# A transformer block's last steps reordered: written order on all engines in the end, a receptance, a key and values in other steps, normalising on VectorE

## The chip, the cores and the metric

The kernel runs on one core of a Trainium2 chip. The metric is device time in microseconds (us) of one execution, start to end; lower is better. A core has TensorE (matrix products and transposes, called PE in the profile), VectorE (DVE), ScalarE (ACT), GpSimd (POOL) and SyncE (SP), which here only issues DMA transfers. Each engine works through its own instructions in their order and waits on semaphores for the others.

## The reference

Eight sequences of 1024 tokens with 256 features, all in float32. A block of two halves, each behind a layer normalisation that is scaled and shifted by a vector of the batch; the gates `ga` and `gb` are vectors of the batch as well:

```python
h = _layernorm(x) * (1 + ca) + sa
x = x + ga * attention(h)          # 16 heads of 16, causal softmax, projection w_out, bias
h = _layernorm(x) * (1 + cb) + sb
# channel mixing; x_prev is h shifted by one token
xr = mu_r * h + (1 - mu_r) * h_prev
xk = mu_k * h + (1 - mu_k) * h_prev
r = sigmoid(xr @ W_r.T)
x = x + gb * r * (square(relu(xk @ W_k.T)) @ W_v.T)
```

## The kernel before

A batch's tokens are cut into two blocks `(b, c)` of 512 (`CW`); a block is four tiles of 128 tokens. The attention is worked through in 32 units `u`, one for four heads of one batch: unit 30 and 31 are the last two of batch 7, so `u // 4` is the batch.

**Steps.** A unit has nine entries (`ORDER`): five pieces along the diagonal (a to e) and four whole tiles of keys (0 to 3). For the last two units other pieces (f, g, h, i) replace b, c and d, so that all of block 0 comes first. A step takes one entry twice: for unit `S`, the *maxima* (`maxima`: products `pp` of queries and keys on TensorE into PSUM, their row maxima on VectorE), and for an earlier entry `T`, nine steps behind (`LAG`), the *weights* (`weights`: products `pw` with the maxima folded in, exponentials on ScalarE, and on GpSimd a select that clears what lies above the diagonal). One entry before `T` is `T1`: at the end of a group of entries, `attend` sums weights times values into `po`. So the steps from 290 to 298 have weights but no maxima, and behind step 298 comes the last `attend`.

When a unit's sums of one block are complete, they have to be divided by the row sums. For units 30 and 31 that is `turn_sums` (four transposes `psum`, a reciprocal and a copy `wide` on VectorE), and one step later `gather_last` (products `pinv`, a multiplication on VectorE, four transfers into `oT`, those of the very last block on the queues of SP and ScalarE alternately).

**Fill.** The rest of the block's work is written into the steps by hand. In `POST_LAST` and `END` an entry `20 x.value0` puts the function `value0` of block `x` twenty steps behind step 261. In `POST_LAST`, `x` and `y` are the two blocks of batch 6; in `END`, `x` and `y` are blocks 0 and 1 of batch 7. A step's fill runs behind its products and before `T1`'s sums; names that begin with `norm` are put ahead of the step's other fill. What a block goes through, in this order: `project0`/`project2` (products `py` with the folded output weights, added to `xb` on VectorE; 0 and 2 are the first of two token tiles), `stats0`/`stats1` (statistics on VectorE, a power and two small multiplications on GpSimd), `norm0`/`norm1` (normalising), `turn` (eight transposes `ptb`, two copies with scale and shift to `h2T`), `mix` (differences of neighbours on GpSimd), four `mixed` (VectorE, into `mix` for the receptance and `step` for the keys), `receptance0`/`2` (products `pr`, tanh on ScalarE to `r`), `key0`/`1` (products `pk`, relu on ScalarE, square on GpSimd to `ka`), `value0`/`2` (`multiplied`: products `pkv`; `valued`: r times them on VectorE, the addition to `xb` on GpSimd, and behind `value2` the transfer to `out`). What `soon` holds is done in a later step, ahead of that step's fill.

In a step with no maxima and no fill TensorE makes five transposes of the identity ("heat").

**Order and banks.** The wrapper `InOrder` ties each instruction to the one before on its engine. TensorE always keeps the written order; the other four keep it where `strict[0]` or `start[0]` is set. `strict[0]` is set in the steps and cleared before the end; there the tile framework's own planner puts the instructions of the four engines in an order. PSUM has four banks tagged `t` (`bank`: pw, po, ptb, psum, pinv) and two double banks tagged `s` (pp). From step 290 on `late[0]` is set, and `bank_apart` (py, pr, pk, pkv, heat) takes its banks from `s`, which no maxima need any more; before it takes them from `t`.

**The end.** `tail` handles block (7, 1) after all steps, in halves of 256 tokens: `project`, `normal`, `turned`, `mixed_half`, `receptance`, `keys`, `values`, with the other block's `multiplied` and `valued` in between. Its tiles end in `_last`. Behind the last sums and before `tail` come `turn_sums`, `gather_last` and the keys of block (7, 0), in the order of `soon`.

Of the kernel before, what the change touches and what calls it, by code (L numbers as in the profile page):

```python
# [8 lines left out]
F32 = mybir.dt.float32  # L9
AF = mybir.ActivationFunctionType  # L10
ALU = mybir.AluOpType
# [3 lines left out]
P = 128  # L15
B, N, D = 8, 1024, 256
H, HD = 16, 16
DC = D // P
CW = 512
NC = N // CW  # L20
# [52 lines left out]
def adaln_block(  # L73
# [89 lines left out]
    def tokens(ap, b, c):  # L163
        return ap[b, c * CW : (c + 1) * CW, :].rearrange("(t p) d -> p t d", p=P)
# [202 lines left out]
    def normalise(xt, S, tag, half):  # L367
        if half == 0:
            S["h"] = sb.tile([P, NT, D], F32, tag="h", bufs=2, name=f"h{tag}")
        h, mv, rs = S["h"], S["mv"], S["rs"]  # L370
        for t in (2 * half, 2 * half + 1):
            if strict[0]:
                act.activation(
                    h[:, t, :],
                    xt[:, t, :],
                    AF.Identity,
                    bias=S["away"][:, t : t + 1],
                    scale=rs[:, t : t + 1],
                )
            else:  # L380
                dve.tensor_scalar(
                    h[:, t, :],
                    xt[:, t, :],
                    mv[:, t, 0:1],
                    rs[:, t : t + 1],
                    ALU.subtract,
                    ALU.mult,
                )

    def transposed(h, to, b, d, shift, scale, name):  # L390

        pt = bank(name)
        for t in range(NT):
            pe.transpose(
                pt[:, t * P : (t + 1) * P], h[:, t, d * P : (d + 1) * P], ident
            )
        by, at = modT[:, scale, d, b : b + 1], modT[:, shift, d, b : b + 1]
        if d and shift == SHIFT_A:
            dve.tensor_scalar(to, pt, by, at, ALU.mult, ALU.add)
        else:  # L400
            act.activation(to, pt, AF.Identity, bias=at, scale=by)
# [363 lines left out]
    def post(b, c):  # L765
# [57 lines left out]
        def receptance(t0):  # L823
            pr = bank_apart(f"pr{b}_{c}_{t0}")
            rows(pr, S["mix"], wr_sb, (t0, t0 + 1))
            r = sb.tile([P, CW], F32, tag="r", bufs=2, name=f"r{b}_{c}_{t0}")
            act.activation(r, pr, AF.Tanh, scale=0.5)
            S["r", t0] = r

# [28 lines left out]
        def tail(other):  # L858

            def both(f):
                f(0)
                f(1)

            def columns(half):
                return slice(half * CW // 2, (half + 1) * CW // 2)

            both(lambda half: project(2 * half))
            other["multiplied0"]()  # L870
            st = sb.tile([P, NT, 6], F32, tag="st", bufs=2, name="st_last")
            mv = sb.tile([P, NT, 2], F32, tag="mv", bufs=2, name="mv_last")
            rs = sb.tile([P, NT], F32, tag="rs", bufs=2, name="rs_last")
            h = sb.tile([P, NT, D], F32, tag="h", bufs=2, name="h_last")

            def normal(half):
                ts = (2 * half, 2 * half + 1)
                for t in ts:
                    dve.bn_stats(st[:, t, :], S["x"][:, t, :])
                    dve.bn_aggr(mv[:, t, :], st[:, t, :])  # L880
                of = slice(2 * half, 2 * half + 2)
                dve.tensor_scalar_add(rs[:, of], mv[:, of, 1], EPS)
                pool.tensor_tensor(rs[:, of], rs[:, of], m_half[:, of], ALU.pow)
                if half:
                    pool.tensor_mul(away, mv[:, of, 0], rs[:, of])
                    pool.tensor_scalar_mul(away, away, -1.0)
                for n, t in enumerate(ts):
                    if half:
                        act.activation(
                            h[:, t, :],  # L890
                            S["x"][:, t, :],
                            AF.Identity,
                            bias=away[:, n : n + 1],
                            scale=rs[:, t : t + 1],
                        )
                        continue
                    dve.tensor_scalar(
                        h[:, t, :],
                        S["x"][:, t, :],
                        mv[:, t, 0:1],  # L900
                        rs[:, t : t + 1],
                        ALU.subtract,
                        ALU.mult,
                    )

            away = sb.tile([P, 2], F32, tag="away", bufs=2, name="away_last")
            both(normal)
            h2T = sb.tile([P, DC, CW + 1], F32, tag="h2T", name="h2T_last")
            pool.tensor_copy(h2T[:, :, 0:1], A[b, 0]["edge"])

            def turned(half):
                pt = bank(f"pt_last{half}")
# [13 lines left out]
                        scale=modT[:, SCALE_B, d, b : b + 1],  # L926
                    )

            turned(0)
            other["multiplied2"]()  # L930
            turned(1)
            step = sb.tile([P, DC, CW], F32, tag="step", name="step_last")
            S["mix"] = sb.tile([P, DC, CW], F32, tag="mix", bufs=2, name="mix_last")

            def mixed_half(half):
                of = columns(half)
                for d in range(DC):
# [5 lines left out]
                for n in range(2):  # L943
                    for d in range(DC):
                        dve.scalar_tensor_tensor(
                            (S["mix"], step)[n][:, d, of],
                            step[:, d, of],
                            mus[:, n, d : d + 1],
                            h2T[:, d, of],
                            ALU.mult,  # L950
                            ALU.add,
                        )

            both(mixed_half)
            other["valued0"](), other["valued2"]()
            S["ka"] = sb.tile([P, DC, CW], F32, tag="mix", bufs=2, name="ka_last")

            def keys(half):
                of = columns(half)
# [11 lines left out]
                act.activation(ka, pk, AF.Relu)  # L971
                dve.tensor_mul(ka, ka, ka)

            both(lambda half: (receptance(2 * half), keys(half)))

            def values(half):
                t0 = 2 * half
                pv = bank(f"pkv_last{half}")
                rows(pv, S["ka"], G[b]["wv"], (t0, t0 + 1))
                r = S["r", t0]  # L980
                dve.scalar_tensor_tensor(r, r, 1.0, pv, ALU.add, ALU.mult)
                dve.tensor_add(flat(t0), flat(t0), r)
                (sync, act)[half].dma_start(
                    tokens(out, b, c)[:, t0 : t0 + 2, :], S["x"][:, t0 : t0 + 2, :]
                )

            both(values)

        return dict(
            load=load_xb,  # L990
# [26 lines left out]

    soon = []

    def step(T, T1, S, now, fill):  # L1020


# [21 lines left out]
        for f in fill:  # L1044
            f()
        if not S and not fill:

            pt = bank_apart(f"heat{now}")
            for n in range(5):
                pe.transpose(pt[:, :P], ident, ident)  # L1050
        if T1 and T1[1] in groups_of(T1[0]):
            finish(T1, now)
        if S:
# [64 lines left out]
    12 y.stats0; 13 x.mixed01; 13 x.mixed10; 13 x.receptance0; 14 x.mixed11; 15 x.receptance2;  # L1118
    15 y.stats1; 16 y.norm0; 17 x.key0; 17 y.norm1; 18 x.key1; 18 y.turn; 19 y.mix; 20 x.value0;
    20 y.mixed00; 21 y.mixed01; 21 y.mixed10; 22 x.value2; 22 y.mixed11; 22 y.receptance0;  # L1120
    23 y.receptance2; 24 y.key0; 25 y.key1; 26 y.value0; 27 y.value2
    """
    PREP = """
    -9 m.stats0; -8 m.stats1; -6 m.norm0; -4 m.norm1; -3 m.turn; -2 n.stats0; 0 n.stats1; 1 m.q0;
# [11 lines left out]
    22 m.k1; 22 n.q1; 24 n.k1; 26 n.v0; 28 n.v2  # L1136
    """
    END = """
    16 x.load; 18 x.bias; 26 y.load; 28 x.project0; 28 y.bias; 29 x.project2; 30 x.stats0;
    30 x.stats1; 31 x.norm0; 32 x.norm1; 32 x.turn; 33 x.mix; 34 x.mixed00; 34 x.mixed01;  # L1140
    34 x.mixed10; 34 x.mixed11; 35 x.receptance0; 36 x.receptance2
    """

    def place(table, at, **of):
# [32 lines left out]
    for b in range(B):  # L1177
# [10 lines left out]
            fold0=lambda b=b: fold(b, 0),  # L1188
            fold1=lambda b=b: fold(b, 1),
        )  # L1190
    place(END, at, x=ready[b][0], y=ready[b][1])


    mask = const.tile([P, CW], F32, tag="mask", name="mask")
# [53 lines left out]
        )  # L1248
    strict[0] = False
    finish(order_t[-1], len(slots))  # L1250
    for n, f in ((1, "key0"), (2, "key1")):
        soon.append((len(slots) + n, ready[B - 1][0][f]))
    soon.sort(key=lambda z: z[0])
    strict[0] = True
# [59 lines left out]
```

## Time and profile before

| | |
|---|---|
| median of 3 runs | 1411.76 us (1409.19 to 1415.02) |
| profiled execution | 1412.37 us, span 1410.7 us, mean granted TensorE clock 0.995 |
| busy: PE, DVE, ACT, POOL | 1382.5, 1063.3, 894.7, 550.9 us |
| step 290 begins (first pw_h) | 1335.64 us |
| last po_i ends | 1374.81 us |
| first py that waits for oT | 1382.79 us |
| last product pkv_last ends | 1405.76 us |
| last transfer to out is issued | 1407.30 us |

The profile is of one execution. Its page gives the span, the busy time of each engine, 40 equal slices of the span and the chain of work that ended last. Beside the page the trace answers with the instructions in order of time (start, length, engine, tile out<-in, shape, count, and in brackets the idle time before and what ended it) and with the busy time of each engine, the granted TensorE clock and the share of the DMA engines in any stretch. Every instruction stands at line 123, that of the wrapper; groups are told apart by their tiles.

### The profile page before, as it was taken

To read this page: it belongs to the slowest core of one execution; us is meant where nothing else is said; L and a number is where in the kernel's file an instruction comes from. 1 tells how busy PE (TensorE), PEld (TensorE's weight loads), DVE (VectorE), ACT (ScalarE), POOL (GpSimd) and SP (SyncE) were. 2 spreads that over 40 slices of the span, in tenths; PEclk is the share of its full clock that TensorE was granted. 3 is DMA by queue.
4 is the path that set the end of the run, shared out by engine and by line. 5 is a ranking of instruction groups with operands and counts; after the bars stand their busy time and mean duration, and the time that the engine had idled before them with its cause. 6 is when DMAs were issued, how large, how long until landed. Compare 5 with 4: busy or idle time off the path is not lost.

```text
span 1410.7 us, 29817 instructions
## 1 busy us (share of the span) xinstructions
PE 1382.5 (98%) x11285; PEld 758.2 (54%) x11285; DVE 1063.3 (75%) x2872; ACT 894.7 (63%) x1695; POOL 550.9 (39%) x841
## 2 busy tenths in 40 slices
PE   9999999999999999999999999999999999989997
PEld 5544555555555555555554555556555555555545
DVE  6777687788777878788877787778887886878524
ACT  3466666666666666666666666666666666566561
POOL 1142242435423454334534355234643344345431
PEclk9999999999999999999999999999999999999999
DMA  6512423222222323223242222323231232301101
GB/s 192 182 36 79 132 77 114 62 97 82 86 79 77 107 70 106 74 66 106 77 129 57 101 84 66 99 77 107 69 104 56 62 107 71 100 24 37 61 5 34
DMA packets 80816, 118.15 MB, mean 84 GB/s; under 512 B 10136, under 2 KB 38680, under 8 KB 80672
## 3 DMA queue, kind: packets, MB, share of 16 engines
q1 hardware_dynamic: 80336, 115.92, 25.4%
q8 instruction: 89, 1.46, 0.4%
q14 instruction: 55, 0.45, 0.1%
q10 hardware_dynamic: 336, 0.33, 0.1%
HBM read 70.63 MB, written 44.55 MB: 82 GB/s over the span
## 4 chain that ended last, share of the span: by engine, by line
PE 91%; DVE 4%; DMA 2%; ACT 2%; POOL 1%; issue 1%; ACTq 0%; SPq 0%; DVEq 0%; POOLq 0%
PE pw L123 12%; PE po L123 8%; PE pp L123 7%; PE pq L123 7%; PE po_c L123 5%; PE po_e L123 5%; PE pr L123 4%; PE py L123 4%; PE pv L123 4%; PE pkv L123 4%; PE pk L123 4%; PE pw_a L123 3%; PE pw_e L123 3%; PE pw_c L123 2%; PE pmx L123 2%; PE pw_b L123 2%
## 5 line engine op out<-in xcount | busy, mean ns | idle before, releaser
L123 DVE TENSOR_REDUCE max<-pp 128x2 f32<-128x1024 f32 x256 | 302.1, 1219 | 65.3 <-PE pp L123 63.1
L123 ACT ACTIVATE w<-pw 128x512 f32<-128x512 f32 x512 | 265.0, 603 | 83.9 <-PE pp L123 60.6
L123 PE MATMUL pw<-q,k 32*128 32x512 f32 x1024 | 265.6, 617 | 0.7 <-ACT w_i L123 0.6
L123 PE MATMUL pp<-k,q 32*128 32x512 f32 x1024 | 256.0, 620 | 0.0
L123 PEld LDWEIGHTS pw<-q,k 32*128 32x128 f32 x1024 | 108.1, 183 | 100.1 <-issue 58.8
L123 DVE DVE_READ_ACCUMULATOR2_ANT max<- 128x1 f32 x1024 | 144.7, 141 | 0.0
L123 DVE CUSTOM_DVE_ANT_0 pp_c<-pp_c,mask 128x256 f32<-128x256 f32 x240 | 102.3, 436 | 46.2 <-PE pp_c L123 40.1
L123 DVE CUSTOM_DVE_ANT_0 pp_b<-pp_b,mask 128x128 f32<-128x128 f32 x240 | 102.4, 437 | 43.8 <-PE pp_b L123 37.5
L123 DVE CUSTOM_DVE_ANT_0 pp_e<-pp_e,mask 128x512 f32<-128x512 f32 x128 | 88.3, 707 | 55.2 <-PE pp_e L123 52.9
L123 PE MATMUL po<-w,v 128*32 128x512 f32 x1024 | 124.7, 605 | 0.0
L123 DVE CUSTOM_DVE_ANT_0 pp_d<-pp_d,mask 128x128 f32<-128x128 f32 x240 | 102.4, 437 | 28.9 <-PE pp_d L123 22.8
L123 PE MATMUL pq<-hT,wqk_sb 128*128 128x512 f32 x240 | 114.0, 607 | 1.0 <-ACT hT L123 1.0
L123 DVE CUSTOM_DVE_ANT_0 pp_a<-pp_a,mask 128x512 f32<-128x512 f32 x128 | 87.8, 707 | 12.6 <-PE pp_a L123 10.4
L123 POOL TENSOR_TENSOR xb<-xb,r 128x512 f32<-128x512 f32 x30 | 41.7, 1390 | 135.1 <-DVE r L123 110.0
L123 ACT ACTIVATE w_a<-pw_a 128x512 f32<-128x512 f32 x128 | 66.3, 603 | 41.6 <-PE pp_a L123 38.5
L123 POOL TENSOR_TENSOR o<-o,more 128x512 f32<-128x512 f32 x62 | 78.6, 1267 | 33.1 <-ACT more L123 33.0
L123 POOL TENSOR_TENSOR rsb<-rsb,m_half 128x2 f32<-128x2 f32 x30 | 21.4, 714 | 175.3 <-DVE rsb L123 174.0
L123 PEld LDWEIGHTS pp<-k,q 32*128 32x128 f32 x1024 | 82.9, 183 | 4.0 <-DVE max L123 3.6
L123 ACT ACTIVATE w_d<-pw_d 128x512 f32<-128x512 f32 x120 | 63.0, 601 | 21.5 <-PE pp_e L123 19.2
L123 ACT ACTIVATE w_e<-pw_e 128x512 f32<-128x512 f32 x128 | 66.1, 605 | 15.7 <-PE pp_c L123 13.5
L123 ACT ACTIVATE w_b<-pw_b 128x512 f32<-128x512 f32 x120 | 62.1, 603 | 18.2 <-PE pp L123 17.6
L123 ACT ACTIVATE w_c<-pw_c 128x512 f32<-128x512 f32 x120 | 62.2, 603 | 15.3 <-PE pp_b L123 10.8
(212 smaller groups left out, 3034.7 us busy)
## 6 DMA issues: line engine op xcount, KB each, us to landing
pad<-qk SPq DMA_DIRECT2D x60, 256.0 KB
q<-pad SPq DMA_DIRECT2D x30, 512.0 KB
k<-pad SPq DMA_DIRECT2D x30, 512.0 KB
od<-o SPq DMA_DIRECT2D x60, 256.0 KB
xa<-in_x SPq DMA_DIRECT2D x16, 512.0 KB
xb<-in_x SPq DMA_DIRECT2D x16, 512.0 KB
oT<-od SPq DMA_DIRECT2D x60, 128.0 KB
ov<-over SPq DMA_DIRECT2D x30, 256.0 KB
```

The lines of the kernel that those rows point to most:

```text
L123: made = f(*args, **kwargs)
```

## The change

In the steps before the end:

- `POST_LAST` (batch 6): receptance0 of block 0 goes from 13 to 14; of block 1, key0 goes from 24 to 26, key1 from 25 to 30, value0 from 26 to 31, value2 from 27 to 33. Numbers from 29 on are steps without maxima.
- `END` (block (7, 0)): statistics, normalisation, turn, mix and mixed go one step earlier, spread a little differently; receptance2 leaves step 297 and is put between `turn_sums` and `gather_last` behind the last sums; key0 and key1 both come behind `gather_last`. `heat` is a function now and is called in step 295 too; 297 and 298 have no fill and so get it as well.
- Where `late[0]` is set, `normalise` uses VectorE and not ScalarE, and the second of a turn's two copies goes to VectorE.

In `tail`:

- `start[0]` is set, so all engines keep the written order.
- Each `normal` follows its `project`; the first half is normalised on ScalarE and the second on VectorE (before it was the other way round).
- `mixed_half` makes a difference and its mix for each feature half in turn; `valued0` and `valued2` of the other block stand behind the first `keys`.
- `late[0]` is cleared behind `turned`, so the receptances take banks tagged `t`; `r` of the last block takes a buffer tagged `w`.
- `values(1)` works in two pieces of one token tile each, with a transfer of its own for each, the last on ScalarE's queue.

```diff
-            if strict[0]:
+            if strict[0] and not late[0]:
                 act.activation(
...
-        if d and shift == SHIFT_A:
+        if d and (shift == SHIFT_A or late[0]):
             dve.tensor_scalar(to, pt, by, at, ALU.mult, ALU.add)
...
-                if half:
+                if half == 0:
                     pool.tensor_mul(away, mv[:, of, 0], rs[:, of])
                     pool.tensor_scalar_mul(away, away, -1.0)
+                    pool.tensor_copy(h2T[:, :, 0:1], A[b, 0]["edge"])
...
+                for ts in ((t0,), (t0 + 1,)) if half else ((t0, t0 + 1),):
+                    of = slice((ts[0] - t0) * D, (ts[-1] + 1 - t0) * D)
+                    rows(pv[:, of], S["ka"], G[b]["wv"], ts)
+                    xs = flat(t0)[:, of]
+                    dve.scalar_tensor_tensor(r[:, of], r[:, of], 1.0, pv[:, of], ALU.add, ALU.mult)
+                    dve.tensor_add(xs, xs, r[:, of])
+                    (act if ts[0] == NT - 1 else sync).dma_start(
...
+            start[0] = True
+            project(0)
+            normal(0)
+            project(2)
+            normal(1)
+            other["multiplied0"]()
+            turned(0)
+            other["multiplied2"]()
+            turned(1)
+
+            late[0] = False
+            mixed_half(0)
+            mixed_half(1)
+            S["ka"] = sb.tile([P, DC, CW], F32, tag="mix", bufs=2, name="ka_last")
+            receptance(0)
+            keys(0)
+            other["valued0"](), other["valued2"]()
+            receptance(2)
+            keys(1)
+            values(0)
+            values(1)
...
-    13 x.receptance0; 14 x.mixed11; 15 x.receptance2;
+    14 x.mixed11; 14 x.receptance0; 15 x.receptance2;
...
-    23 y.receptance2; 24 y.key0; 25 y.key1; 26 y.value0; 27 y.value2
+    23 y.receptance2; 26 y.key0; 30 y.key1; 31 y.value0; 33 y.value2
...
-    16 x.load; 18 x.bias; 26 y.load; 28 x.project0; 28 y.bias; 29 x.project2; 30 x.stats0;
-    30 x.stats1; 31 x.norm0; 32 x.norm1; 32 x.turn; 33 x.mix; 34 x.mixed00; 34 x.mixed01;
-    34 x.mixed10; 34 x.mixed11; 35 x.receptance0; 36 x.receptance2
+    16 x.load; 18 x.bias; 26 y.load; 28 x.project0; 28 y.bias; 29 x.stats0; 29 x.project2;
+    30 x.stats1; 30 x.norm0; 31 x.norm1; 31 x.turn; 32 x.mix; 32 x.mixed00; 33 x.mixed01;
+    33 x.mixed10; 33 x.mixed11; 34 heat; 35 x.receptance0
...
-    for n, f in ((1, "key0"), (2, "key1")):
+    for n, f in ((1, "receptance2"), (2, "key0"), (2, "key1")):
         soon.append((len(slots) + n, ready[B - 1][0][f]))
```

More of the change, by code (lines that the diff above doesn't have):

```diff
@@ L825, in receptance @@
             rows(pr, S["mix"], wr_sb, (t0, t0 + 1))
-            r = sb.tile([P, CW], F32, tag="r", bufs=2, name=f"r{b}_{c}_{t0}")
+            name = f"r{b}_{c}_{t0}"
+            if (b, c) == (B - 1, NC - 1):
+                r = sb.tile([P, 2, CW], F32, tag="w", bufs=8, name=name)[:, 0, :]
+            else:
+                r = sb.tile([P, CW], F32, tag="r", bufs=2, name=name)
             act.activation(r, pr, AF.Tanh, scale=0.5)
@@ L858, in tail @@
         def tail(other):
-            def both(f):
-                f(0)
-                f(1)
             def columns(half):
                 return slice(half * CW // 2, (half + 1) * CW // 2)
-            both(lambda half: project(2 * half))
-            other["multiplied0"]()
             st = sb.tile([P, NT, 6], F32, tag="st", bufs=2, name="st_last")
@@ L873, in tail @@
             rs = sb.tile([P, NT], F32, tag="rs", bufs=2, name="rs_last")
+            away = sb.tile([P, 2], F32, tag="away", bufs=2, name="away_last")
             h = sb.tile([P, NT, D], F32, tag="h", bufs=2, name="h_last")
+            h2T = sb.tile([P, DC, CW + 1], F32, tag="h2T", name="h2T_last")
+            step = sb.tile([P, DC, CW], F32, tag="step", name="step_last")
+            S["mix"] = sb.tile([P, DC, CW], F32, tag="mix", bufs=2, name="mix_last")
             def normal(half):
@@ L883, in normal @@
                 pool.tensor_tensor(rs[:, of], rs[:, of], m_half[:, of], ALU.pow)
-                if half:
+                if half == 0:
                     pool.tensor_mul(away, mv[:, of, 0], rs[:, of])
                     pool.tensor_scalar_mul(away, away, -1.0)
+                    pool.tensor_copy(h2T[:, :, 0:1], A[b, 0]["edge"])
                 for n, t in enumerate(ts):
-                    if half:
+                    if half == 0:
                         act.activation(
@@ L904, in normal @@
                     )
[L906 to L909, printed above, removed]
             def turned(half):
@@ L927, in turned, with one @@
                     )
[L929 to L933, printed above, removed]
             def mixed_half(half):
                 of = columns(half)
+                def one(n, d):
+                    dve.scalar_tensor_tensor(
+                        (S["mix"], step)[n][:, d, of],
+                        step[:, d, of],
+                        mus[:, n, d : d + 1],
+                        h2T[:, d, of],
+                        ALU.mult,
+                        ALU.add,
+                    )
                 for d in range(DC):
@@ L942, in mixed_half @@
                     )
[L943 to L956, printed above, removed]
+                    one(0, d)
+                one(1, 0), one(1, 1)
             def keys(half):
@@ L972, in keys @@
                 dve.tensor_mul(ka, ka, ka)
-            both(lambda half: (receptance(2 * half), keys(half)))
             def values(half):
@@ L978, in values @@
                 pv = bank(f"pkv_last{half}")
-                rows(pv, S["ka"], G[b]["wv"], (t0, t0 + 1))
                 r = S["r", t0]
[L981 to L987, printed above, removed]
+                for ts in ((t0,), (t0 + 1,)) if half else ((t0, t0 + 1),):
[5 more added lines that the diff above has]
+                    (act if ts[0] == NT - 1 else sync).dma_start(
+                        tokens(out, b, c)[:, ts[0] : ts[-1] + 1, :],
+                        S["x"][:, ts[0] : ts[-1] + 1, :],
+                    )
+            start[0] = True
[18 more added lines that the diff above has]
+            values(1)
         return dict(
@@ L1018, in adaln_block, with heat @@
     soon = []
+    def heat():
+        pt = bank_apart(f"heat{clock[0]}")
+        for n in range(5):
+            pe.transpose(pt[:, :P], ident, ident)
     def step(T, T1, S, now, fill):
@@ L1046, in step @@
         if not S and not fill:
-            pt = bank_apart(f"heat{now}")
-            for n in range(5):
-                pe.transpose(pt[:, :P], ident, ident)
+            heat()
         if T1 and T1[1] in groups_of(T1[0]):
@@ L1117, in adaln_block @@
     9 x.norm0; 9 y.project0; 10 x.norm1; 10 x.turn; 11 x.mix; 11 y.project2; 12 x.mixed00;
-    12 y.stats0; 13 x.mixed01; 13 x.mixed10; 13 x.receptance0; 14 x.mixed11; 15 x.receptance2;
+    12 y.stats0; 13 x.mixed01; 13 x.mixed10; 14 x.mixed11; 14 x.receptance0; 15 x.receptance2;
     15 y.stats1; 16 y.norm0; 17 x.key0; 17 y.norm1; 18 x.key1; 18 y.turn; 19 y.mix; 20 x.value0;
     20 y.mixed00; 21 y.mixed01; 21 y.mixed10; 22 x.value2; 22 y.mixed11; 22 y.receptance0;
-    23 y.receptance2; 24 y.key0; 25 y.key1; 26 y.value0; 27 y.value2
+    23 y.receptance2; 26 y.key0; 30 y.key1; 31 y.value0; 33 y.value2
     """
@@ L1190, in adaln_block @@
         )
-    place(END, at, x=ready[b][0], y=ready[b][1])
+    place(END, at, x=ready[b][0], y=ready[b][1], heat=heat)
     mask = const.tile([P, CW], F32, tag="mask", name="mask")
```

## The prediction

> **What bounds the kernel now.** I read the page first, then the instructions of each engine in order of time from 1195 us to the end, then the granted clock in slices of 1 us, because nearly all edits lie behind 1255 us. The page (span, busy time, the 40 slices, the chain that ended last):
>
> ```profile
> span 1410.7 us, 29817 instructions
> PE 1382.5 (98%) x11285; PEld 758.2 (54%) x11285; DVE 1063.3 (75%) x2872; ACT 894.7 (63%) x1695; POOL 550.9 (39%) x841
> PE   9999999999999999999999999999999999989997
> PE 91%; DVE 4%; DMA 2%; ACT 2%; POOL 1%; issue 1%; ACTq 0%; SPq 0%; DVEq 0%; POOLq 0%
> ```
>
> TensorE is 91% of the chain, so an idle hole on it in the middle is time lost, and the last slices (8, 9, 9, 9, 7) are where it isn't full. A busy PE in these rows includes matmuls that wait for a bank, so I look at the instructions. TensorE around 1260 and 1320 us (start, length, what; in brackets the idle time before and who ended it), with VectorE's rows between:
>
> ```profile
> 1258.36 0.70 PE L123 MATMUL pr<-wr_sb,mix 128*128 128x256 f32 x2
> 1260.79 1.56 PE L123 MATMUL pr<-wr_sb,mix 128*128 128x256 f32 x6 [1.73 <-DVE mix L123]
> ...
> 1257.69 2.36 DVE L123 TENSOR_REDUCE max<-pp 128x2 f32<-128x1024 f32 x2 [0.79 <-PE pp L123]
> 1259.97 0.77 DVE L123 SCALAR_TENSOR_TENSOR mix<-step,mus,h2T 128x512 f32<-128x512 f32 x1
> ...
> 1317.60 1.88 PE L123 MATMUL pk<-step,wk_sb 128*128 128x512 f32 x4
> 1322.34 1.89 PE L123 MATMUL pkv<-wvb,ka 128*128 128x256 f32 x8
> 1327.94 1.99 PE L123 MATMUL pkv<-wvb,ka 128*128 128x256 f32 x8
> ```
>
> The receptance of step 274 stops TensorE for 1.73 us until its mix is made. The three lower groups are key1 and both values of batch 6, in steps where TensorE has no hole. Then the steps without maxima (290 to 298, from 1335.64 to 1374.81) and the end:
>
> ```profile
> 1341.06 2.27 PE L123 MATMUL pw<-q,k 32*128 32x512 f32 x8 [0.62 <-ACT w_i L123]
> 1353.49 2.08 PE L123 MATMUL pinv<-ident,wide 128*128 128x128 f32 x8
> 1355.50 3.49 PE L123 MATMUL po<-w,v 128*32 128x512 f32 x16
> 1365.17 1.92 PE L123 MATMUL po<-w,v 128*32 128x512 f32 x16
> ...
> 1352.00:1353.00 1.00, 1.00 (x3) 0.00 (x0) 0.00 (x0) 1.00 (x3) 1.00 (x2) 0.50 0.00 0
> ...
> 1389.47 1.23 DVE L123 TENSOR_SCALAR rs_last<-mv_last 128x2 f32<-128x2 f32 x1
> 1392.33 1.09 ACT L123 ACTIVATE h_last<-xb,away_last,rs_last 128x256 f32<-128x256 f32 x2 [2.78 <-POOL away_last L123]
> 1392.98 1.40 PE L123 MATMUL pt_last<-ident,h_last 128*128 128x128 f32 x4 [2.83 <-ACT h_last L123]
> 1407.30 0.43 ACTq L123 DMA_DIRECT2D out<-xb  x1
> ```
>
> The same 16 matmuls of po take 1.92 us and, at a granted clock of 0.50 (the number after the engines' five columns), 3.49 us. In the end the second half's normalisation comes 4 us late: its tiny rs_last ran 1.23 us instead of the first half's 0.17, beside GpSimd's 1.45 us addition of a value to xb, and TensorE stood 2.83 us.
>
> **The change part by part**, against the profiled execution (1412.37 us, span 1410.7; 0.6 us above the median of the three runs).
>
> *A, receptance0 of batch 6 from step 274 to 275.* Its 1.73 us hole goes. Late next are the maxima: the second product of step 275 needs the bank that VectorE's second reduction frees at 1257.69 + 2.36 = 1260.05, where TensorE alone would be there 0.3 us earlier. Then mix is ready (1260.74) before the receptance comes up. Gain 1.45; bounds 0.7 (both products wait a whole reduction) and 1.73.
>
> *B, steps 285 to 289.* key0 moves from 285 to 287, the same work. key1 leaves 286 (start to next start 1317.60 to 1319.41: 1.81), value0 leaves 287 (1322.34 to 1324.16: 1.82), value2 leaves 288 (1327.94 to 1329.87: 1.93): 5.56 us. Step 288 keeps only products and weights, 1.93 us on TensorE, beside two reductions of 2.36 in all, so 289 waits 0.5 for banks. project0 of the last batch then comes up some 5 us earlier, but what it reads (four transfers of oT, issued one after the other by SP from 1323.65 to 1326.79) hangs on step 287's pinv and moves up about 3 us: a margin that was 5 us shrinks to 3 after issue, no wait. Gain 5.0; bounds 3.5 (three steps bound by VectorE, and a short wait for oT) and 5.56.
>
> *C, steps 290 to 298.* Before, they take 1374.81 − 1335.64 = 39.17 us. Full-clock work in them, by rows: weights 7.3, sums po and po_i 8.3, receptances 3.6, projection 1.8, transposes, pinv and heat 3.6, so 25 us; the other 14 are waits and the half clock (2.08 − 1.05 for pinv, 3.49 − 1.92 for po: 2.6). The change puts batch 6's key1, value0 and value2 in (3 × 1.75), takes block (7,0)'s receptance2 out (1.75, to where its key0 stood behind the last sums; key0 moves to key1's place behind pinv, and key1 into the wait for oT, 1380.9 to 1382.79) and adds two heat groups (0.66 each). So the question is how much of it fits. Step by step, in us from the start of 290:
> - 290: 3.87 as before (pw_h's fourth bank, maxima row, projection). stats0 runs on VectorE in it, its power on GpSimd ends at 3.86.
> - 291: weights 0.9, key1 1.75: 6.5. It covers the 0.62 wait for ACT's exponentials. norm0 is two VectorE instructions of 0.41 instead of two ACT ones of 0.55.
> - 292: weights 0.9, value0 1.75 and 0.5 of waiting for GpSimd's square of key1 (1.04, behind two selects of 0.64); queued behind it on TensorE are the transposes of turn and po_i. Transposes 1.1 (norm1 ready by then), po_i 2.3: 13.05. The second turned copy goes to VectorE, 0.81 for ACT's 0.72, in parallel.
> - 293: weights 1.6 (the fourth bank waits for ACT's copy of po_i), sums turned 0.9: 15.55. Before, ACT's 2.2 us of normalising stood in front of these exponentials.
> - 294: weights 1.6, pinv 1.1, value2 1.75, po 1.85: 21.85.
> - 295: weights 1.6, heat 0.65: 24.1. 296: weights 1.8, receptance0 1.75, po 1.85: 29.5. 297: 1.4 and 0.65: 31.55. 298: 1.45, 0.65, and 2.3 for po_i behind the selects: 35.95.
>
> That is 3.2 us less than 39.17, though 5.25 us of work came in. The mixes on VectorE may be held by GpSimd's additions (the longest mix row, 2.78 us for 0.72, ends as such an addition does); receptance0 has 2 us to spare. On SP the output of block (6,1) now queues behind four oT transfers, with nothing behind it before step 301. Bounds: 0.6 with one more stretch at half clock as long as before's (2.6), 5 if the bank waits are half mine.
>
> Here the row and a rule differ. Row: the clock fell at 1351.9, and TensorE had no idle gap over 0.75 us in the 3.4 us before, but transposes and waits for ACT. The Trainium skill, "TensorE: Matmul & The Clock Gate", asks in its part on the clock gate for a whole idle window of 3.4 us, and says in its part on transposes that they don't count as busy in the same way. By the first the new steps stay at full clock; by the second heat, five transposes, helps nothing, and steps 293 to 297 could fall to half speed, which leaves C at 0.6.
>
> *D, the end.* Up to py nothing moves: between the last sums and pinv stands receptance2 (1.72) instead of key0 (1.72), and py waits for oT as before, until 1382.79 on before's time. From there, on that time:
> - First half: power on GpSimd to 1387.07, two small multiplications (0.65, as at 1391.66 to 1392.31), ACT's two normalisations from 1387.74 to 1388.83, transposes to 1389.35, ACT's two copies to 1390.45: 0.9 later than before.
> - Second half: xb at 1386.85, statistics 1.25, power 0.72, VectorE's two of 0.41: ready at 1389.7 instead of 1393.42. Its transposes follow multiplied2 at 1391.07; copies end at 1392.65 instead of 1395.44.
> - VectorE then makes each half in six instructions at a pitch of 0.40: first mix ready 1391.6, second step 1394.95. TensorE runs from 1391.65 without a hole: four groups of 1.73, values(0) to 1400.3, values(1) after a 0.3 wait for the square (GpSimd's two additions hold it) to 1402.1. Before: 1405.76. The valued pair now waits behind the mixes and the first square; only its own output waits on it.
> - Last: 256-wide pieces, 0.45 and 0.40 for 0.69 and 0.69: VectorE ends at 1403.3 instead of 1407.27; the last transfer is half as large but shares the queues with 768 KB more within 4 us.
>
> Gain 4.2; bounds 2.7 (the end's first products at half clock as at 1393) and 5.
>
> Sum: 1.45 + 5.0 + 3.2 + 4.2 = 13.85; 1412.37 − 13.85 = 1398.5, and on the median some 1398.
>
> **The rivals.** *Cold stretches remain* in C and D: 1.45 + 5.0 + 0.6 + 2.7 = 9.75, so 1402. For it: two fell before, and the phase is free. Against: fewer waits for ACT. 20%. *The late steps have no room*: the 14 us of waits stay whole, and what enters (5.25 + 1.3 − 1.75 = 4.8) is added, less the 2.6 of half clock: C is −2.2, the sum 8.45, the time 1403.5; if a cold stretch comes too, 1406. For it: banks, not TensorE, set the pace of 292 to 294. Against: keys and values use the other banks, which maxima have left. 14%. *The written order changes nothing on VectorE and the end stays* (the wait is GpSimd's, not the order's): D falls to 1 by the shorter last pieces, 1402 again; 7%. *Slower:* TensorE stays at half clock from 297 to the end, since heat is transposes: receptance2, keys, projections and values there are 22 us of full-clock rows, so +22 against 13.85, about 1420. It decides from 14 us of such work, eight windows; before's stretches were one and two windows. 3%.
>
> **How the numbers follow.** My forecast has 56%. All bounds at their best give a gain of 17.3, at their worst 7.5, so 1394.5 to 1404.5 on the median; with the no-room case beside a cold stretch it reaches 1406. About 0.5% (7 us) is what a measurement of this kernel can tell from no change (its three runs span 5.8): below 1404.7 I see 0.86, within it 0.1, slower 0.04.
>
> **What would show it.** Right: no DVE-mix wait at pr near 1260; step 290's pw_h near 1329; 36 us from there to the last po_i; the second half's pt_last 1.5 us behind its pkv instead of 2.8; some 24 us from the py that waits for oT to the end of the span instead of 27.9. Wrong: a granted clock of 0.50 anywhere behind 1330, pw waiting over 2 us in 292 to 294, py waiting in step 289.

## The result and the profile after

The changed kernel takes 1403.68 us (median of six runs, 1401.08 to 1407.10), the kernel before 1411.84 us in the same comparison (six runs, 1409.19 to 1415.02). The ratio is 0.9942 with a 95% interval of [0.9924, 0.9961]: 8.2 us less, between 5.5 and 10.7. The forecast was 1398.0 us; the time lies inside its range of 1394 to 1406, and of the forecast gain of 13.85 us some 59% came. Two runs at a mean granted clock under 0.95 (1445.38 us in *e1_end_only*, 1556.91 us in *e5_act_norm*) are left out of all medians and ratios here.

The profiled execution took 1404.88 us. The page of after, the span, the busy times, TensorE's 40 slices, and the chain that ended last:

```profile
span 1403.1 us, 29835 instructions
PE 1380.6 (98%) x11295; PEld 758.8 (54%) x11295; DVE 1067.7 (76%) x2879; ACT 893.1 (64%) x1690; POOL 550.3 (39%) x841
PE   9999999999999999999999999999999999999998
PE 91%; DVE 3%; DMA 2%; ACT 1%; POOL 1%; issue 1%; SPq 0%; ACTq 0%; DVEq 0%; POOLq 0%
```

TensorE's last slices are 9, 9, 9, 9, 8 where they were 8, 9, 9, 9, 7. VectorE has 4.4 us more work, ScalarE 1.6 less. The time is read best in the four parts of the prediction: A from the start of step 274 to that of 285, B from there to 290, C from there to the end of the last po_i, D from there to the end of the span. The second column is another profile of the kernel before (experiment *e9_before_again* below), in which the granted clock never fell behind step 274; the third is what the prediction expected of after.

| us | before, first profile | before, again | expected of after | after |
|---|---|---|---|---|
| ahead of step 274 | 1256.43 | 1256.49 | 1256.43 | 1259.56 |
| A | 52.67 | 52.69 | 51.22 | 51.53 |
| B | 26.53 | 26.53 | 21.53 | 22.26 |
| C | 39.17 | 35.91 | 35.95 | 37.29 |
| D | 35.84 | 34.48 | 31.64 | 32.51 |

**A and B.** TensorE (PE) and VectorE (DVE) of after, in order of time:

```profile
1264.29 1.99 PE L123 MATMUL pr<-wr_sb,mix 128*128 128x256 f32 x8
...
1326.10 4.81 DVE L123 TENSOR_REDUCE max<-pp 128x2 f32<-128x1024 f32 x4 [3.72 <-PE pp L123]
...
1329.56 1.99 PE L123 MATMUL py<-wob,oT 128*128 128x256 f32 x8
```

The receptance, now in step 275, has no bracket: its wait of 1.73 us for the mix is gone. In steps 288 and 289 VectorE reduces for 4.81 us without a pause while TensorE has little beside the products and weights, so VectorE sets the pace there. project0 (py) follows without a wait: the transfers into oT landed in time.

**C**, on TensorE and ScalarE, the groups of weights pw behind a po:

```profile
1353.93 1.92 PE L123 MATMUL po<-w,v 128*32 128x512 f32 x16
1355.78 1.90 PE L123 MATMUL pw<-q,k 32*128 32x512 f32 x8
1355.92 0.59 ACT L123 COPY o<-po 128x512 f32<-128x512 f32 x1 [3.40 <-PE po L123]
1357.00 2.06 ACT L123 ACTIVATE w<-pw 128x512 f32<-128x512 f32 x4 [0.49 <-PE pw L123]
1358.31 1.93 PE L123 MATMUL pw_e<-q,k 32*128 32x512 f32 x8
```

Eight pw are 1.14 us of TensorE where nothing holds them (a row of *e3* below); here they take 1.90, though TensorE shows as busy: the last two wait for the fourth bank, which ScalarE's copy of po leaves at 1356.51.

**D**, on all engines, the second half's normalisation and the last values:

```profile
1383.70 1.09 ACT L123 ACTIVATE h_last<-xb,away_last,rs_last 128x256 f32<-128x256 f32 x2 [4.88 <-POOL away_last L123]
1384.36 0.33 PE L123 MATMUL pt_last<-ident,h_last 128*128 128x128 f32 x1 [0.76 <-ACT h_last L123]
1385.13 0.74 DVE L123 TENSOR_SCALAR h_last<-xb,mv_last,rs_last 128x256 f32<-128x256 f32 x2 [0.85 <-POOL rs_last L123]
1386.96 0.60 PE L123 MATMUL pt_last<-ident,h_last 128*128 128x128 f32 x4
...
1397.73 0.41 DVE L123 SCALAR_TENSOR_TENSOR r<-r,pkv_last 128x256 f32<-128x256 f32 x1
...
1398.20 1.13 PE L123 MATMUL pkv_last<-wvb,ka_last 128*128 128x256 f32 x4 [0.73 <-DVE r L123]
1399.37 0.42 DVE L123 SCALAR_TENSOR_TENSOR r<-r,pkv_last 128x256 f32<-128x256 f32 x1 [0.76 <-PE pkv_last L123]
```

The second half's transposes (1386.96) follow with no wait; the 2.83 us is gone, and what is left is 0.76 us for the first half. But there is a new wait of 0.73 us, in the last product: its second piece waits until VectorE has read the first.

### The profile page after: what moved, and what is told of

Read it like the earlier page. It is cut to its first block, busy times and chain, and to the rows that moved or that the text cites. A ratio compares the mean times of both kernels' runs of the same rounds, so it can differ in the third digit from the quotient of the medians.

```text
span 1403.1 us, 29835 instructions
## 1 busy us (share of the span) xinstructions
PE 1380.6 (98%) x11295; PEld 758.8 (54%) x11295; DVE 1067.7 (76%) x2879; ACT 893.1 (64%) x1690; POOL 550.3 (39%) x841
## 4 chain that ended last, share of the span: by engine, by line
PE 91%; DVE 3%; DMA 2%; ACT 1%; POOL 1%; issue 1%; SPq 0%; ACTq 0%; DVEq 0%; POOLq 0%
PE pw L123 12%; PE po L123 8%; PE pp L123 7%; PE pq L123 7%; PE po_c L123 5%; PE po_e L123 5%; PE py L123 4%; PE pr L123 4%; PE pkv L123 4%; PE pk L123 4%; PE pv L123 4%; PE pw_a L123 3%; PE pw_c L123 3%; PE pw_e L123 3%; PE pmx L123 2%; PE pw_b L123 2%
```

## The experiments

Each is the changed kernel with one edit, where nothing else is said. Parts A to D repeated within some 0.05 us from profile to profile of equal code, as long as the granted clock stayed at 1.00, so one profile can tell a part's length; times need several runs.

### The kernel before, profiled again

An unchanged kernel, to see what of C and D in the first profile was the clock.

> The kernel before once more, for a second profile. The profile shown first had two stretches at half clock behind step 290 (6.8 and 3.4 us long). Theory 1 (they are the execution's chance, and the forecast counted them as the kernel's): without them the stretch from step 290 to the last po_i is 36 to 37 us instead of 39.2 and the end 34 to 35 instead of 35.8. Theory 2 (the waits of these steps bring them in every execution): the same stretches at 0.50 and the same times.

It took 1407.82 us; C was 35.91 and D 34.48. The same stretch of time in the first profile of before and in this one (columns: busy time of PE, PEld, DVE, ACT, POOL with instructions, then the granted clock, the DMA share and GB/s):

```profile
1353.00:1355.00 2.00, 2.00 (x8) 1.51 (x8) 0.00 (x0) 0.88 (x2) 0.85 (x1) 0.50 0.00 0
```

```profile
1353.00:1355.00 2.00, 2.00 (x20) 1.17 (x23) 0.96 (x2) 0.85 (x2) 0.92 (x1) 1.00 0.00 0
```

Same code at the same place, the start of step 290 0.07 us apart: once at 0.50 with 8 matmuls, once at 1.00 with 20. So 39.17 − 35.91 = 3.26 us of C and 35.84 − 34.48 = 1.36 us of D, 4.6 in all, belonged to that one execution and not to the kernel. Against this profile the change gives A 1.16, B 4.27, C −1.38 and D 1.97: 6.0 us, and C is a loss (it took in 5.25 us of products). The four expected parts lie 9.3 us under it, so at equal clock the forecast was 9.3 and 6.0 came.

The end of before at full clock, TensorE in this profile:

```profile
1379.59 3.26 PE L123 MATMUL py<-wob,oT 128*128 128x256 f32 x14 [1.71 <-DMA oT<-o]
...
1389.79 0.33 PE L123 MATMUL pt_last<-ident,h_last 128*128 128x128 f32 x1 [2.83 <-ACT h_last L123]
...
1397.57 3.63 PE L123 MATMUL pkv_last<-wvb,ka_last 128*128 128x256 f32 x16
```

The last product ends 4.90 us ahead of the end of the span (1406.11); in after it is 3.82. So of D's 1.97 us, 1.08 lie behind the last product, where the last piece and its transfer are now half as large, and only 0.88 ahead of it: the 2.83 us went, but after has new waits of 0.76 and 0.73, and its last sixteen products, parted by the second wait, take 4.12 us of TensorE for 3.63. That py no longer waits for oT is worth nothing: its last product ends 11.23 us behind the last po_i here and 11.24 in after, because receptance2, put behind the last sums, takes the time of the wait.

### The end alone

The kernel before with the new `tail` and nothing else of the change.

> The kernel before with the changed end alone (tail, and r of the last block in a w buffer); steps as before. Theory 1 (the parts add up and each was sized too large): the stretch from the last sums' addition to the end falls from 35.8 to about 32.4 us as in the changed kernel, time 3 to 4 us under before, ratio 0.9975. Theory 2 (the end gains only because the moved receptance and keys leave it covered): it stays above 34.5 us and the time within 1.5 us of before.

Five rounds gave 1409.24 us (eleven runs) against 1410.28, ratio 0.9994 [0.9981, 1.0007]: no difference to be measured. For a profile at full clock behind step 274 the same kernel was run once more:

> The kernel before with the changed end alone, once more, for a profile at full clock (the profile of the first was of an execution whose clock was granted at 0.949 throughout). Theory 1 (the end's own gain is the difference at full clock, 34.5 to 32.5): from the last po_i to the end 32 to 32.7 us. Theory 2 (the gain needs the moved receptance): 33.5 or more. Every timed run of it had a mean clock under 0.999, so a stretch at 0.50 is expected somewhere behind step 290, and with it a longer stretch from there to the last po_i than the 35.9 of before at full clock.

1408.45 us, A 52.67, B 26.53, C 35.91 as before, and D 32.49: the end alone takes 1.99 us off at full clock, all of D's gain. The stretch at half clock that I expected behind 290 did not come (two came early, at 37 and 102 us). The medians of the timed runs don't show the 2 us; their mean granted clock was 0.996, that of the 26 runs of before 0.997, and what the clock takes is of that size. A straight line through the eleven times against the clock comes to 1404.6 us at 1.000, the one for before to 1407.3 (last section): 2.7 us less. That is an estimate, since none of the eleven ran above 0.998.

### The end in the planner's order

```diff
-            start[0] = True
             project(0)
             normal(0)
```

> The changed kernel without the written order on VectorE, ScalarE, GpSimd and SP in the end: the planner orders them as before the change. Theory 1 (the order is what removed the late second normalisation): a valued product and its addition on GpSimd come ahead of the second half's statistics again, TensorE waits 2 us or more for pt_last and the end is 34 us or longer. Theory 2 (the exchange of the halves and the later call of valued did it): the end stays within 0.7 us of 32.4.

1402.50 us, ratio 0.9942 [0.9926, 0.9958], D 32.52: equal to after. From its trace, VectorE, GpSimd and TensorE:

```profile
1382.27 1.27 POOL L123 TENSOR_TENSOR xb<-xb,r 128x512 f32<-128x512 f32 x1
...
1382.34 1.67 DVE L123 TENSOR_SCALAR h_last<-xb,mv_last,rs_last 128x256 f32<-128x256 f32 x2 [0.23 <-POOL rs_last L123]
...
1384.38 0.60 PE L123 MATMUL pt_last<-ident,h_last 128*128 128x128 f32 x4
```

The planner brings a valued forward again, and h_last takes 1.67 us beside GpSimd's addition (0.74 in after). But with the normalisations placed behind their projections and the second on VectorE, that fits into TensorE's 1.89 us of multiplied2: the transposes have no wait. The written order itself is worth nothing. What removed the 2.83 us is among the other edits of `tail`: the exchange of the halves, each `normal` behind its `project`, the later call of `valued`; no run separates them.

### A bank for each piece of the last values

```diff
-                pv = bank(f"pkv_last{half}")
                 for ts in ((t0,), (t0 + 1,)) if half else ((t0, t0 + 1),):
+                    pv = bank(f"pkv_last{ts[0]}")
```

> The changed kernel, with a bank of its own for each piece of the end's values. In the changed kernel the last 4 products stand 0.73 us behind VectorE's reading of the piece before in the same bank, with another 0.4 us of matmul tail. Theory 1 (the shared bank is the missing 0.8 us of the end's forecast): that wait is gone and the end is 31.6 us instead of 32.4. Theory 2 (it is VectorE's queue that sets the end): the products end earlier, but VectorE's last addition moves by less than 0.3 us.

1402.33 us, ratio 0.9946 [0.9927, 0.9964], which alone says nothing of a microsecond; D is 31.64, 0.87 less. TensorE's last group in it:

```profile
1397.14 3.85 PE L123 MATMUL pkv_last<-wvb,ka_last 128*128 128x256 f32 x16
```

All sixteen run in one go. The new wait came from the two pieces sharing a bank.

### po in the double banks

```diff
-        po = bank(f"po{u}_{k}")
+        po = bank_apart(f"po{u}_{k}")
```

> The changed kernel, with the sums po of the steps without maxima in the banks that the maxima have left. Theory 1 (in these steps the fourth bank of pw waits for ScalarE's copy of po; that is what the forecast of 36 us undersized): each pw behind a po takes 0.9 to 1.1 instead of 1.7 to 1.9 us, 3 to 4 times, and the stretch from step 290 to the last po_i falls from 37.3 to about 34.5 us; time 2 to 3 us under the changed kernel. Theory 2 (ScalarE's exponentials set the pace): pw waits for them instead and the stretch stays above 36.5.

1402.77 us, ratio 0.9951 [0.9937, 0.9966]; C 37.27, unchanged. TensorE and ScalarE, the place shown of after:

```profile
1356.44 1.14 PE L123 MATMUL pw<-q,k 32*128 32x512 f32 x8
...
1357.66 2.06 ACT L123 ACTIVATE w<-pw 128x512 f32<-128x512 f32 x4 [0.50 <-PE pw L123]
1358.31 2.59 PE L123 MATMUL pw_e<-q,k 32*128 32x512 f32 x8
```

pw no longer waits (1.14 for 1.90), but the next step's pw_e takes 2.59 for 1.93: it meets ScalarE's exponentials of the four banks before. Taking po out of the way only moved the wait, so the copy of po alone is not what limits. What is left is the round from pw through four exponentials and back to the bank; *e8_best* below tests it.

### ScalarE normalises again in the late steps

```diff
-            if strict[0] and not late[0]:
+            if strict[0]:
...
-        if d and (shift == SHIFT_A or late[0]):
+        if d and shift == SHIFT_A:
```

> The changed kernel with the normalising and the second turned copy of the steps without maxima on ScalarE again. Theory 1 (ScalarE, 2.2 us of normalising ahead of the exponentials, set these steps' pace): the stretch from step 290 to the last po_i rises from 37.3 to 39 us or more. Theory 2 (the round of pw, its exponentials and the banks they free sets it, and the wait for GpSimd's power is there on either engine): it stays below 38.

C 38.56, between what the two theories asked for: VectorE's share is worth 1.27 us. The time was 1404.15 us (three runs), ratio 0.9955 [0.9928, 0.9982].

### Key and values back in their old steps

```diff
-    23 y.receptance2; 26 y.key0; 30 y.key1; 31 y.value0; 33 y.value2
+    23 y.receptance2; 24 y.key0; 25 y.key1; 26 y.value0; 27 y.value2
```

> The changed kernel with batch 6's key0, key1 and both values at their old places, in steps 285 to 288. Steps 285 to 289 then take 26.5 us again instead of 22.3 by both theories. Theory 1 (the steps without maxima have room for the 5.25 us of products): from step 290 to the last po_i it falls by less than 3 us, so the moving gains 1.3 us or more. Theory 2 (no room, they only change places): it falls by 4 us or more, to 33 or less, and the moving gains nothing.

B 26.53 (+4.27), C 34.10 (−3.19); 1403.71 us, ratio 0.9956 [0.9941, 0.9971]. 5.25 us of products cost the late steps 3.19, so the move gains 1.08 net; that lies between the two theories, and the times (1403.71 us against after's 1403.68) can't show it. And without the products C is 1.81 shorter than before's 35.91: that is what normalising on VectorE, the receptance's move and the rest of `END` give.

### No heat

The three calls of `heat` in steps 295, 297 and 298 (transposes whose result nothing uses) are left out: the rule in `step` and the entry in `END`.

> The changed kernel without any heat group. Theory 1 (transposes don't keep the clock up, and the groups lie in waits): no granted clock of 0.50 from step 290 on, the stretch to the last po_i 36.5 to 37.4 us against 37.3. Theory 2 (heat is what keeps the clock): a stretch at 0.50 between step 294 and the end, and 1.5 to 3 us more.

Step 296 began 0.67 us earlier (24.30 for 24.97 from the start of 290), but the clock fell in step 298 and C was 38.73, 1.44 longer. The stretches of its trace, columns as above:

```profile
1365.00:1366.00 1.00, 0.57 (x4) 0.19 (x8) 0.00 (x0) 1.00 (x4) 0.26 (x1) 0.78 0.00 0
1366.00:1367.00 1.00, 1.00 (x8) 0.27 (x4) 0.00 (x0) 0.44 (x2) 0.88 (x2) 0.50 0.00 0
...
1368.00:1369.00 1.00, 1.00 (x12) 0.54 (x8) 0.00 (x0) 0.00 (x0) 0.00 (x0) 0.51 0.00 0
```

The longest idle time of TensorE in the steps before was 0.53 us. The time, 1403.73 us, ratio 0.9954 [0.9938, 0.9970], can't be told from after's.

### More banks for the weights

The runs point to the round of pw. So the second pair of pw goes into the double banks and the fill into the banks tagged `t` while the steps run; besides, the values get a bank for each piece, and the turn of block (6, 0) comes one step later, where TensorE had waited 1.51 us for its last hb (a wait that before has too).

```diff
+        if late[0] and half:
+            two = ps_s.tile([P, 2, CW], F32, tag="s", name=f"pw{u}_{k}_{half}")
+            pw = [two[:, 0, :], two[:, 1, :]]
...
-        if late[0]:
+        if late[0] and behind[0]:
             return ps_s.tile([P, 2, CW], F32, tag="s", name=name)[:, 0, :]
...
-    9 x.norm0; 9 y.project0; 10 x.norm1; 10 x.turn; 11 x.mix; 11 y.project2; 12 x.mixed00;
+    9 x.norm0; 9 y.project0; 10 x.norm1; 11 x.turn; 11 x.mix; 11 y.project2; 12 x.mixed00;
```

> The changed kernel with three edits: a bank of its own for each piece of the end's values; the turn of batch 6's first block one step later (in the changed kernel TensorE stands there 1.5 us for ScalarE's normalising, at step 271); in the steps without maxima the second half of pw in the double banks that the maxima have left, the fill in the other four, so that half of a step's weights never wait for the exponentials of the step before. Theory 1 (those exponentials and the banks they hold set the pace): the stretch from step 290 to the last po_i falls from 37.3 to 32 to 35 us; the end to 31.6; 1.5 us less ahead of step 274: 4 to 7 us under the changed kernel. Theory 2 (TensorE and the chain through po set it): the stretch stays above 36.5 and all is 2 to 3 us under the changed kernel.

1396.31 us (1394.51 to 1397.02), ratio 0.9898 [0.9883, 0.9912]. C is 33.40 and D 31.65. TensorE in the same place (the wrapper is line 124 here), and two waits that are left:

```profile
1344.47 0.66 PE L124 MATMUL psum<-ident,o 128*128 128x128 f32 x4 [0.98 <-POOL o L124]
...
1350.80 1.14 PE L124 MATMUL pw<-q,k 32*128 32x512 f32 x8
...
1352.57 1.24 PE L124 MATMUL pw_e<-q,k 32*128 32x512 f32 x8
...
1364.17 0.66 PE L124 MATMUL psum<-ident,o 128*128 128x128 f32 x4 [0.85 <-DVE o L124]
```

Both pw and pw_e run at TensorE's own pace now: the additional banks took 3.89 us off C (the other two edits lie ahead of step 274 and in D), so the round was what limited.

### The transposes of the sums covered, with and without heat

On top of it, VectorE adds po to the sums directly in the late steps (no copy by ScalarE, no addition by GpSimd), and receptance2 is cut in two, one piece ahead of psum:

```diff
-        elif strict[0]:
+        elif strict[0] and not late[0]:
             more = sb.tile([P, CW], F32, tag="more", bufs=2, name=f"more{u}_{k}")
...
-    for n, f in ((1, "receptance2"), (2, "key0"), (2, "key1")):
+    for n, f in ((0, "receptance2a"), (1, "receptance2b"), (2, "key0"), (2, "key1")):
```

> The best kernel so far (ratio 0.990), with two edits: half of the last receptance2 ahead of psum, where TensorE stands 0.85 us for VectorE's addition, and half behind; in the steps without maxima VectorE adds po to the sums in one instruction of 0.69 us, instead of ScalarE's copy (0.58) and GpSimd's addition (1.27), for which psum waits 0.98 us in step 293. Theory 1 (both waits are on the path): 33.4 from step 290 to the last po_i falls to 32.4, the end from 31.65 to 30.9, the time to about 1394.5. Theory 2 (another wait takes their place): less than 0.6 us in all.

1394.06 us (1392.72 to 1397.71), ratio 0.9880 [0.9856, 0.9905]; C 32.56, D 31.09, and both groups of psum run without a wait:

```profile
1341.17 0.66 PE L124 MATMUL psum<-ident,o 128*128 128x128 f32 x4
...
1361.12 0.60 PE L124 MATMUL psum<-ident,o 128*128 128x128 f32 x4
```

The same without heat:

> The kernel of the run before in this call without any heat group, three in these steps (0.7 us each). Theory 1 (heat holds the clock; without it the changed kernel fell to 0.50 in step 298): a stretch at 0.50 behind step 294 again, and the time 1 us or more above. Theory 2 (with fewer waits TensorE's products alone hold the clock): no such stretch, and up to 2 us less.

1394.08 us, ratio 0.9875 [0.9849, 0.9900]: the same time. C is 31.46, 1.10 less, and in its profile the clock did not fall behind 290. These two are the best versions found, some 17 us under the kernel before by their ratios.

## Why the prediction was right, and where not

The direction stands, A and B lie within their bounds, and D's main wait went as worked out; C lost where a gain was forecast. The profiled execution of after took 1404.88 us where the sum said 1398.5; the 6.4 us between are 0.31 in A, 0.73 in B, 1.34 in C, 0.87 in D, and 3.13 ahead of step 274, where the code is unchanged.

That the time lies inside the range is partly luck. At equal clock the parts gained 6.0 us, less than the 7.5 of all bounds at their worst; 1411.84 − 6.0 would have been 1405.8, inside only because the range went on to 1406. And 1403.7 is nearer to the numbers of two rivals, 1402 with cold stretches and 1403.5 with no room, than to 1398, though no half clock came behind step 274 in after's profile. None of the signs of being wrong came: the pw of 292 to 294 took at most 1.90 us, and py did not wait in step 289.

- **A**: the step is right. 1.16 us for 1.45, within its bounds.
- **B**: 4.27 for 5.0, within its bounds. The term that was too small is the time that VectorE keeps for itself: step 287 took 7.05 us where about the same work had taken 6.60 before, and 289 took 6.64 where 5.77 and a wait of 0.5 were expected. oT came in time, as worked out.
- **C**: this step failed, in two ways. Its size: I gave each group of pw in 293 to 295 1.6 us, and they took 1.8 to 1.9, in all 0.73 us more over the three steps; 296 and 297 added 0.50 and 291 0.15, which is the 1.34 to within 0.04. The bank waits were seen, but taken as one late bank each; *e3* and *e8* show a round through four exponentials that limits every late step. And its sign: 39.17 contained 3.26 us at half clock that the kernel need not have (the prediction put 2.6 on it, and saw that "the phase is free"), yet I subtracted from 39.17 and took the difference as a gain of the change. Against 35.91 the part is 1.38 longer. The rival of no room was half right: of 5.25 us, 3.19 were added (*e7*).
- **D**: the wait's mechanism held: the first half's work came later and the second half's wait went. But at equal clock the gain is 1.97 us, under the lower bound of 2.7. Of the 4.2, 1.36 were half clock, of the same kind as in C, and 0.87 is the bank that the two last pieces share, which was not in the sum: with a bank each *e2* reaches the expected 31.64. Behind the last product the change gave 1.08, more than the 0.5 us that the sum had for it. The rival that the order does nothing on VectorE was right on the order (*e4*) and wrong that the end would stay.
- **What a median contains.** I took a stretch at half clock out of before's execution and left none in after's, ahead of step 274 or behind. At a mean granted clock of 1.000, three runs of before took 1406.95, 1407.53 and 1407.82 us and one of after 1401.08: 5.9 to 6.7 apart, where A to D make 6.0. The rest of the measured 8.2 probably goes with the clock: the six runs of after had 0.998 on the mean, the 50 of before in the comparisons of the experiments 0.997, with medians of 1409.9 to 1410.3 us; for the six that gave 1411.84 no clock is on record. That the change itself lowers the share of half clock is not shown, since stretches come and go in equal code.
- **The clock's rule.** The prediction weighed a row against the Trainium skill, "TensorE: Matmul & The Clock Gate": a whole idle window of 3.4 us in the part on the clock gate. TensorE's longest idle time behind its first products was 2.83 us (near its end, at 1392.84, the clock fell in before, and not in *e9_before_again*, which had the same stall), and it fell at places with far shorter ones. The same page has a section that fits better and that I passed over, "A second HAM failure mode: psum-queue depth-cycling": in a bf16 kernel that cycles through its PSUM banks, short idle times between groups of products come often enough to let the clock swing. Before's first stretch behind 290, the one at 1351.9 among pw that wait for banks (longest idle time ahead of it 0.75 us), fits that in kind, and so does *e6*'s in step 298 (0.53 us); here the products are float32. *e9_before_again* had the same waits and no fall, so the waits alone don't decide it. On transposes, which that page says don't count as busy in the same way, the runs are split: without heat the clock fell in *e6* and not in *e11*, one profile each, so whether heat holds the clock stays open. The three runs of *e6* all had a mean granted clock of 0.997, the three of *e7* in the same comparison 0.998, which fits one more stretch in each without heat but doesn't show it. The 3% given to half clock through the whole end was not tested further; no profile shows it.

## What to carry to other kernels

Before a part of a profile is subtracted from, its granted clock has to be 1.00, or a second profile of the same kernel taken: here 4.6 us of a forecast gain of 13.9 were an accident of one execution. Where TensorE is "busy" with few matmuls for its time, follow the whole round of a bank (product, exponentials, back) before moving work in: only more banks in that round gave the time back, not taking one user away. And two pieces that are meant to overlap, one written while the other is read, gained 0.87 us here from a bank each.

## What the hardware showed that was not expected

- Through 50 runs of the kernel before (all those in the experiments' comparisons but one), a straight line of time against mean granted clock gives 1407.3 us at 1.000 and 1.1 us more for each 0.001 below; for the other kernels with five runs or more the line has 1.1 to 1.6. Most of the spread between executions goes with this. Apart from the first 10 us and what lies behind the last products, half clock came in stretches of 3.4 or 6.8 us (*e1_end_only*'s profile aside). In after's, one began at 1249.8 and cost 1.05 us (9.23 us in before from the first pw_c to step 274, 10.28 here), behind a wait of 1.51 us that other profiles have with no fall behind it.
- VectorE instructions beside a GpSimd addition took up to seven times as long: rs_last 1.23 us for 0.17 beside one of 1.45, the pair of h_last 1.67 for 0.74 beside one of 1.27. In *e4* that cost nothing, because TensorE had other work for as long.
- TensorE waited 0.73 us to write one half of a PSUM bank while VectorE read the other half; with two banks there was no wait. Whether the hardware needs that wait or only the framework's bookkeeping asks for it, no run here tells.
